# Loads back from DRAM set apart from their stores on one DMA queue, in a two-layer graph kernel

## The chip, the cores and the metric

The kernel runs on one core of a Trainium2 chip. The metric is the device time of one execution in microseconds (us), the median of several runs. The engines are named as in the profile: PE (matrix products), PEld (its weight loads), DVE, ACT and POOL (elementwise work), and SP, which does no arithmetic here and issues every DMA; SPq is its queue.

## The reference

128 graphs of 128 nodes with 256 features each go through two layers. All data are float32.

```python
# layer 0: two graph attention passes, then a feed-forward block
Wh = h @ W;  e = leaky_relu(Wh @ a1 + (Wh @ a2).T, 0.2)
att = softmax(where(adj > 0, e, NEG), axis=1);  h = att @ Wh          # twice
h = layernorm(x + h);  x = layernorm(h + relu(h @ wf1 + bf1) @ wf2 + bf2)
# layer 1: 8-head attention with one value matrix per relation r, then a feed-forward block
attn = softmax(q @ k.T / sqrt(32))
out = sum over r of (attn * (adj == r)) @ (x @ Wv[r] + bv[r])
x = layernorm(x + out @ Wo + bo)
return layernorm(x + gelu(x @ W1 + b1) @ W2 + b2)
```

The adjacency holds zeros and ones. A test on the device finds that and takes the arm of the program called `BINARY`, in which two of the four relations are enough.

## The kernel before

**Groups and stages.** Four graphs make a group (`G = 4`), and there are 32 groups. Each goes through five stages: `load`, `gat` (both attention passes of layer 0), `ff0`, `att` (the attention of layer 1) and `ff1`. A stage is a Python generator: it emits some instructions, yields a number, and is resumed later. The planner in `layers` keeps all generators in a heap, ordered by a time of its own: a group's stages begin at `PERIOD * g` plus a fixed offset (`begin`, 48 for `ff0`, 132 for `att`, 300 for `ff1`; the period is 100), and each yielded number is the distance to the next step. These numbers, in the table `TIMES`, are plan units and not microseconds. So several groups are in work at once, and the steps of different groups interleave.

**What the order of emission fixes.** SP's instructions stay in the order of emission throughout, PE's from plan time 280 on (`kept`). The order on DVE, ACT and POOL is chosen by the framework's scheduler, by priority and by its own estimate of times.[...]

**Trips through DRAM.** PE multiplies over partitions, so some tiles must be turned. In the first and the last group this is done by PE (`direct`). In the others DVE turns blocks of 32x32 in place, four stores write the tile to a DRAM buffer `zd` with the blocks in their new places, and one load brings it back (`transposed`, lines 288 to 293):

```python
nc.vector.transpose(z, y)
s = dr.tile([n, N, NQ, Q], F32, name="zd", bufs=8)
for i in range(NQ):
    nc.sync.dma_start(s[:, :, i]..., z[ts(i, Q)]...)
nc.sync.dma_start(t, s.rearrange("k p i t -> p k (i t)"))
```

The load waits for the four stores to have landed, on SP. A group makes seven such trips of 512 KB: features ahead of `ff0`, `att` and `ff1` (`features`, tile `T`), and the attention weights of its four graphs (`turned`, tile `e` to `eT`). A smaller trip spreads a row of layer 0's scores over all partitions, twice a group: one store to `zsd` and one load into `e` (`gat_weighting`, lines 405 and 407).

**The attention stage.** `weights(b)` makes the scores of graph b (L490), their row maxima (L496), exponentials (L500) and, on POOL, the division (L502). The plan then has `turned` for graph 0, a step of 5, `turned` for graph 1, a step of 5.5, then the values of graph 0 (`v`, PE L531 and DVE L532) and the masked weights (`m`, DVE L515, from `eT` and the mask `am`). `weighted` (L544, tile `av`) multiplies `v` with `eT` and `m`: the first product of a graph with the weights that made the trip. In the loop over the four graphs the values, output projection (L577), `turned` and `m` of later graphs follow one another.

**Around it.** POOL also does the gains and offsets of the layer norms (`affine`, L271), sums for the feed-forward blocks (L309 to L312, L352), and small steps of the norms (L259 to L263).

Of the kernel before, what the change touches and what calls it, by code (L numbers as in the profile page):

```python
# [24 lines left out]
P = 128  # L25
G = 4
# [2 lines left out]

TIMES = {  # L30
    "sums": 5, "ff visits": (2.5, 2.5, 3, 3, 3.25, 3.25, 3.25, 3.25), "ff2": 3,
    "ff first half": 10, "ff half": 5, "row": 16, "gat": 19, "wh": 5.5,
    "gat copy": 2, "qk": 4.5, "scores": 5.5, "turn0": 10, "turn1": 5,
    "v0": 5.5, "av": 9, "v": 4, "wo": 4, "turn": 3, "mask": 3,
    "lead ff0": 26, "lead att": 32, "lead ff1": 32, "affine": 7,
    "store": 25,
}
STAGES = "load", "gat", "ff0", "att", "ff1"
# [182 lines left out]
def stages_of(tc, a, out, c, pools, plan):  # L221

    nc = tc.nc
    TIMES, binary = plan["times"], plan["binary"]
# [6 lines left out]
    DC, R, MW = c.DC, c.R, c.MW  # L231
# [38 lines left out]
        for op, v in zip((OP.mult, OP.add), c.ln[k]):  # L270
            engine.tensor_tensor(y[:, b:b + n], y[:, b:b + n], v[:, None, :].to_broadcast([P, n, D]), op)  # L271

    def transposed(y, t, direct, z):

        n = y.shape[1]
        if direct:
            for k in range(0, n, G):
                p = ps.tile([P, G, N], F32, name="mm")  # L280
                for b in range(G):
                    nc.tensor.transpose(p[:, b], y[:, k + b], c.ident)  # L282
                if k:
                    nc.vector.tensor_copy(t[:, k:k + G], p)
                else:
                    nc.scalar.copy(t[:, k:k + G], p)
            return
        nc.vector.transpose(z, y)
        s = dr.tile([n, N, NQ, Q], F32, name="zd", bufs=8)
        for i in range(NQ):  # L290
            nc.sync.dma_start(s[:, :, i].rearrange("k (j a) t -> a (k j) t", a=Q),  # L291
                              z[ts(i, Q)].rearrange("a k (j t) -> a (k j) t", t=Q))
        nc.sync.dma_start(t, s.rearrange("k p i t -> p k (i t)"))

    def t_tile():
        return wk.tile([P, G * MW], F32, name="T", bufs=TB)[:, :G * D]
# [1 line left out]
    def features(y, direct):  # L298

        t = t_tile().rearrange("p (b c n) -> p b c n", b=G, c=DC)  # L300
        blocks = t.rearrange("p b c n -> p (b c) n")
        transposed(y.rearrange("p b (c f) -> p (b c) f", f=P), blocks, direct, blocks)
        return t

    def moving_sums(hT):
# [9 lines left out]
    def feed_forward(y, before, direct, win, bin_, wout, func, by=G):  # L315


        hT = features(y, direct)
        yield TIMES["lead ff0" if before == "01" else "lead ff1"]
        hs = moving_sums(hT)  # L320
        yield TIMES["sums"]
        fT = [None] * FC

        def unit(f0):

            lo, hi = (wk.tile([P, 2, 2, T // 2], F32, name="fT", bufs=FC // 2) for _ in range(2))
            for i in range(2):
                fT[f0 + i] = lo[:, i].rearrange("p h t -> p (h t)")
                fT[FC // 2 + f0 + i] = hi[:, i].rearrange("p h t -> p (h t)")

            def product(p, k, first=False):
                for i in range(2):
                    nc.tensor.matmul(p[:, i], win[k][:, ts(f0 + i, P)], hs[k], start=first and i == 0, stop=True,  # L333
                                     skip_group_check=True)

            chain, side = (ps.tile([P, 2, T // 2], F32, name="mm") for _ in range(2))
            product(chain, 1, True)
            product(side, 5, True)
            nc.scalar.copy(lo[:, :, 0], chain)
            nc.scalar.copy(hi[:, :, 0], side)  # L340
            yield
            p = ps.tile([P, 2, T // 2], F32, name="mm")
            product(chain, 6)
            product(p, 2, True)
            product(side, 3)
            nc.scalar.copy(lo[:, :, 1], chain)
            nc.vector.tensor_add(lo[:, :, 0], lo[:, :, 0], p)
            nc.vector.tensor_add(lo[:, :, 1], lo[:, :, 1], side)  # L348
            yield
            product(chain, 7)  # L350
            nc.scalar.copy(hi[:, :, 1], chain)  # L351
            nc.gpsimd.tensor_add(hi[:, :, 1], hi[:, :, 1], hi[:, :, 0])  # L352
            for i in range(2):
                nc.scalar.activation(lo[:, i], lo[:, i], func, bias=bin_[:, f0 + i:f0 + i + 1])  # L354
            yield
            product(chain, 4)
            for h, p in enumerate((chain, hi[:, :, 1])):
                for i in range(2):
                    f = FC // 2 + f0 + i
                    nc.scalar.activation(hi[:, i, h], p[:, i], func, bias=bin_[:, f:f + 1])  # L360
            yield

        units = [unit(0), unit(2)]
        for n, now in enumerate(((0,), (1,), (0,), (1,), (0,), (1,), (0,), (1,))):
            for u in now:
                next(units[u])
            if n in (2, 4):
                affine(y, before, n - 2, 2)
            yield TIMES["ff visits"][n]
        yield TIMES["ff2"]  # L370

        late = sorted(range(FC), key=lambda f: f % (FC // 2) // 2)
        ys = [ps.tile([P, 2, D], F32, name="mm") for _ in range(G // 2)]

        def second(b, part):

            for n, f in part:
                nc.tensor.matmul(ys[b // 2][:, b % 2], fT[f][:, ts(b, N)], wout[:, f],  # L378
                                 start=b % 2 == 0 and n == 0, stop=n == FC - 1, skip_group_check=True)

        order = list(enumerate(late))
        for b in range(G):
            second(b, order[:FC // 2])
        yield TIMES["ff first half"]
        for k in range(0, G, 2):
            for b in (k, k + 1):
                second(b, order[FC // 2:])
            nc.vector.tensor_add(y[:, k:k + 2], y[:, k:k + 2], ys[k // 2])
            yield TIMES["ff half"]
            if (k + 2) % by == 0:  # L390
                normalised(y, k + 2 - by, by)
        return y

    def gat_weighting(wh, k, cap, direct):

        e = wk.tile([P, G, N], F32, name="e")
        if direct:
            p = ps.tile([P, G, N], F32, name="mm")
            for b in range(G):
                nc.tensor.transpose(p[:, b], wh[:, b, k + 1:k + 2].to_broadcast([P, N]), c.ident)  # L400
        else:
            z = sm.tile([P, G, Q], F32, name="zs", bufs=2)
            nc.vector.transpose(z, wh[:, :, k + 1:k + 2].to_broadcast([P, G, Q]))
            s = dr.tile([G, NQ, Q], F32, name="zsd")
            nc.sync.dma_start(s.rearrange("b i t -> i b t"), z[::Q])
            p = e
            nc.sync.dma_start(p, bass.AP(tensor=s.tensor, offset=s.offset, ap=[[0, P], [1, G * N]]))
        yield TIMES["row"]
        for b in range(G):
            nc.scalar.activation(e[:, b], p[:, b], AF.Identity, bias=wh[:, b, k:k + 1])  # L410

        n = 2 if direct else G
        parts = [slice(b, b + n) for b in range(0, G, n)]
        nm = sm.tile([P, G], F32, name="nm")
        s = sm.tile([P, G], F32, name="s")
        for k in parts:
            nc.vector.scalar_tensor_tensor(e[:, k], e[:, k], ALPHA, e[:, k], op0=OP.mult, op1=OP.max)
            nc.vector.scalar_tensor_tensor(e[:, k], cap[:, k], BIG, e[:, k], op0=OP.subtract, op1=OP.min)
            nc.vector.tensor_reduce(nm[:, k], e[:, k], AX.X, OP.max, negate=True)  # L419
        for k in parts:  # L420
            for b in range(k.start, k.stop):
                nc.scalar.activation(e[:, b], e[:, b], AF.Exp, bias=nm[:, b:b + 1], accum_out=s[:, b:b + 1])  # L422
            nc.vector.reciprocal(s[:, k], s[:, k])  # L423
            nc.gpsimd.tensor_mul(e[:, k], e[:, k], per_row(s[:, k], N))  # L424
        return e
# [32 lines left out]

    def attention(y, g, first, direct):

        hT = features(y, first or direct)
        at = load_mask(g)
        yield TIMES["lead att"]
        qT = t_tile().rearrange("p (c t) -> p c t", c=DC)
        for i in range(DC):
            p = ps.tile([P, T], F32, name="mm")
# [37 lines left out]

        def turned(e):
            eT = wk.tile([P, H, N], F32, name="eT")
            transposed(e, eT, direct, e)
            return eT

        def by_relation(b, eT, parts):  # L510

# [45 lines left out]
        eT = [turned(es[0])]  # L557
        yield TIMES["turn1"]
        eT.append(turned(es[1]))
        yield TIMES["v0"]  # L560
        PARTS = range(R)
        v, ms = values(0), by_relation(0, eT[0], range(R))
        for b in range(G):
            more = b + 1 < G
            affine(y, "02", b, 1)
            yield TIMES["av"]
            oT = weighted(ms, v)

            if b + 2 < G:
# [11 lines left out]
                eT.append(turned(es[b + 2]))  # L581
            yield TIMES["mask"]
            if more:
                ms = by_relation(b + 1, eT[b + 1], range(R))
        yield 1
        normalised(y)
        return y
# [195 lines left out]
```

## Time and profile before

| | |
|---|---|
| time, median of 3 runs | 2887.8 us (2886.82 to 2892.35) |
| profiled execution, span | 2890.0 us, mean clock of PE 0.982 |
| busy | PE 2787.7, PEld 2166.1, ACT 1724.3, POOL 1597.4, DVE 1504.7 us |
| the 16 DMA engines | busy for 49% of the span, 113 GB/s |
| stores of trips | 496 of `e` and 364 of `T`, 128 KB each |
| loads of trips | 124 of `eT` and 91 of `T`, 512 KB each |
| SP's queue waiting for stores of `e`, `T`, `zs` to land | 327.3, 228.4 and 197.9 us |

A busy PE isn't a PE at its peak, since products overlap. The idle time of an engine matters only where it delays another that sets the end. In a timeline, each line gives the start, the length, the engine or queue, the line of the kernel, the operation, what it writes and reads, and in brackets how long the engine had stood idle and for what. The profile numbers tiles away, so `eT` stands for the tiles of all graphs.

### The profile page before, as it was taken

To read this page: it belongs to the slowest core of one execution; us is meant where nothing else is said; L and a number is where in the kernel's file an instruction comes from. 1 tells how busy PE (TensorE), PEld (TensorE's weight loads), DVE (VectorE), ACT (ScalarE), POOL (GpSimd) and SP (SyncE) were. 2 spreads that over 40 slices of the span, in tenths; PEclk is the share of its full clock that TensorE was granted. 3 is DMA by queue.
4 is the path that set the end of the run, shared out by engine and by line. 5 is a ranking of instruction groups with operands and counts; after the bars stand their busy time and mean duration, and the time that the engine had idled before them with its cause. 6 is when DMAs were issued, how large, how long until landed. Compare 5 with 4: busy or idle time off the path is not lost.

```text
span 2890.0 us, 45554 instructions
## 1 busy us (share of the span) xinstructions
PE 2787.7 (96%) x15554; PEld 2166.1 (75%) x15554; DVE 1504.7 (52%) x3072; ACT 1724.3 (60%) x5191; POOL 1597.4 (55%) x1866
## 2 busy tenths in 40 slices
PE   4996999999999999999999999999999999999988
PEld 3764777777877777777777787777778777777756
DVE  5444545545545555554554555555565545555442
ACT  3445566566666666666656666666666675666543
POOL 1434556556655556665655665565566565556553
PEclk7998999999999999999999999999999999999999
DMA  7145454555554556555445545454654544564310
GB/s 275 45 104 121 104 118 106 110 132 127 119 114 107 113 117 139 114 119 118 106 108 131 129 113 125 104 111 117 137 128 107 123 106 111 122 135 106 77 37 15
DMA packets 1156945, 328.69 MB, mean 114 GB/s; under 512 B 903008, under 2 KB 1126752, under 8 KB 1156064
## 3 DMA queue, kind: packets, MB, share of 16 engines
q1 hardware_dynamic: 1156704, 325.68, 49.1%
q8 instruction: 126, 2.06, 0.3%
q14 instruction: 115, 0.94, 0.1%
HBM read 195.97 MB, written 129.62 MB: 113 GB/s over the span
## 4 chain that ended last, share of the span: by engine, by line
PE 71%; DMA 7%; DVE 6%; POOL 5%; ACT 4%; issue 2%; SPq 2%; DVEq 0%; POOLq 0%; ACTq 0%
PE mm L378 25%; PE mm L333 19%; PE mm L531 5%; PE mm L474 4%; PE mm L468 4%; PE mm L490 4%; PE av L544 3%; PE mm L435 3%; PE mm L577 3%; POOL tok L271 2%; DMA zd<-e 2%; SPq L291 2%; DMA eT<-zd 2%; PE mm L454 1%; DMA zd<-T 1%
## 5 line engine op out<-in xcount | busy, mean ns | idle before, releaser
L271 POOL TENSOR_TENSOR tok<-tok,ln_rows 128x512 f32<-128x512 f32 (+1 forms) x596 | 669.5, 1133 | 34.4 <-PE mm L282 11.1
L500 ACT ACTIVATE e<-mm,nm 128x128 f32<-128x128 f32 x1024 | 362.1, 397 | 239.2 <-DVE nm L496 229.6
L378 PE MATMUL mm<-w,fT 128*128 128x256 f32 x2048 | 460.6, 381 | 0.0
L378 PE MATMUL mm<-wf,fT 128*128 128x256 f32 x2048 | 456.6, 381 | 1.5 <-ACT fT L354 1.5
L378 PEld LDWEIGHTS mm<-w,fT 128*128 128x128 f32 x2048 | 386.6, 190 | 74.2 <-issue 24.2
L502 POOL TENSOR_TENSOR e<-e,s 128x512 f32<-128x512 f32 x256 | 269.4, 1053 | 300.5 <-DVE s L501 299.8
L378 PEld LDWEIGHTS mm<-wf,fT 128*128 128x128 f32 x2048 | 386.5, 190 | 64.3 <-issue 9.2
L515 DVE TENSOR_TENSOR m<-eT,am 128x1024 f32<-128x1024 f32 x128 | 186.2, 1454 | 385.2 <-DMA eT<-zd 374.8
L496 DVE TENSOR_REDUCE nm<-mm 128x4 f32<-128x512 f32 x256 | 162.9, 676 | 254.6 <-PE mm L490 254.6
L265 ACT ACTIVATE tok<-tok,nmr,rstd 128x256 f32<-128x256 f32 x480 | 249.9, 603 | 20.1 <-POOL nmr L263 20.0
L531 PE MATMUL mm<-wv,T 128*128 128x512 f32 x512 | 249.3, 610 | 0.0
L352 POOL TENSOR_TENSOR fT<-fT 128x512 f32<-128x512 f32 x128 | 163.3, 1277 | 153.8 <-ACT fT L351 153.8
L500 ACT ACTIVATION_READ_ACCUMULATOR e<-mm,nm 128x1 f32 x1024 | 242.9, 237 | 0.0
L354 ACT ACTIVATE fT<-fT,col 128x512 f32<-128x512 f32 x256 | 170.4, 715 | 118.8 <-DVE fT L348 117.1
L309 POOL TENSOR_TENSOR t<-T 128x256 f32<-128x256 f32 x64 | 47.6, 744 | 321.3 <-DMA T<-zd 321.0
L333 PE MATMUL mm<-T,w 128*128 128x256 f32 x768 | 202.3, 386 | 4.0 <-DMA T<-zd 2.9
L424 POOL TENSOR_TENSOR e<-e,s 128x512 f32<-128x512 f32 (+1 forms) x68 | 68.1, 1002 | 244.4 <-DVE s L423 230.6
L333 PE MATMUL mm<-T,wf 128*128 128x256 f32 x768 | 193.1, 381 | 0.0
L256 DVE BATCH_NORM_STATS2 st<-tok 128x6 f32<-128x256 f32 x480 | 176.7, 409 | 2.4
L333 PEld LDWEIGHTS mm<-T,w 128*128 128x128 f32 x768 | 144.4, 192 | 30.6 <-issue 6.5
L422 ACT ACTIVATE e<-e,nm 128x128 f32<-128x128 f32 x256 | 101.6, 430 | 105.2 <-DVE nm L419 98.8
L333 PEld LDWEIGHTS mm<-T,wf 128*128 128x128 f32 x768 | 146.1, 191 | 21.7 <-issue 0.8
(144 smaller groups left out, 5147.1 us busy)
## 6 DMA issues: line engine op xcount, KB each, us to landing
zd<-e SPq DMA_DIRECT2D x496, 128.0 KB, 4.6
eT<-zd SPq DMA_DIRECT2D x124, 512.0 KB, 4.4
zd<-T SPq DMA_DIRECT2D x364, 128.0 KB, 3.5
T<-zd SPq DMA_DIRECT2D x91, 512.0 KB, 4.2
xt<-in_xT_dram SPq DMA_DIRECT2D x32, 512.0 KB, 5.0
e<-zsd SPq DMA_DIRECT2D x60, 256.0 KB, 3.3
tok<-in_x_dram SPq DMA_DIRECT2D x30, 512.0 KB
out_dram<-tok SPq DMA_DIRECT2D x29, 512.0 KB, 5.4
```

Source lines behind the costliest of these rows:

```text
L256: nc.vector.bn_stats(st, y[:, b])
L265: nc.scalar.activation(y[:, b], y[:, b], AF.Identity, bias=nmr[:, b:b + 1], scale=rstd[:, b:b + 1])
L271: engine.tensor_tensor(y[:, b:b + n], y[:, b:b + n], v[:, None, :].to_broadcast([P, n, D]), op)
L333: nc.tensor.matmul(p[:, i], win[k][:, ts(f0 + i, P)], hs[k], start=first and i == 0, stop=True, skip_group_check=True)
L352: nc.gpsimd.tensor_add(hi[:, :, 1], hi[:, :, 1], hi[:, :, 0])
L354: nc.scalar.activation(lo[:, i], lo[:, i], func, bias=bin_[:, f0 + i:f0 + i + 1])
L378: nc.tensor.matmul(ys[b // 2][:, b % 2], fT[f][:, ts(b, N)], wout[:, f], start=b % 2 == 0 and n == 0, stop=n == FC - 1, skip_group_check=True)
L496: nc.vector.tensor_reduce(nm, p, AX.X, OP.max, negate=True)
L500: nc.scalar.activation(eh[:, q], p[:, q], AF.Exp, bias=nm[:, q:q + 1], accum_out=s[:, q:q + 1])
L502: nc.gpsimd.tensor_mul(eh, eh, per_row(s, N))
L515: nc.vector.tensor_tensor(m, eT, at[:, b][:, None, :].to_broadcast([P, H, N]), OP.mult)
L531: nc.tensor.matmul(p, hT[:, b, f], wv[:, f, r:r + 2], start=f == 0, stop=f == DC - 1)
```

## The change

Each trip is emitted in two steps. `transposed` becomes `put`, which turns and stores, and a new `get` emits the load, 4 to 6 plan units later. The numbers in `TIMES` that followed a trip are smaller by what the new steps take, so that everything else keeps its plan time. The aim is that SP doesn't have to wait for the stores to land before it issues what comes next. In `attention` the load of graph 0 is emitted behind the stores of graph 1, that of graph 1 one step later; the loads of graphs 2 and 3 get a step of their own in the loop.

```diff
@@ -29,10 +29,10 @@
 
 TIMES = {
     "sums": 5, "ff visits": (2.5, 2.5, 3, 3, 3.25, 3.25, 3.25, 3.25), "ff2": 3,
-    "ff first half": 10, "ff half": 5, "row": 16, "gat": 19, "wh": 5.5,
+    "ff first half": 10, "ff half": 5, "row": 12, "gat": 19, "wh": 5.5,
     "gat copy": 2, "qk": 4.5, "scores": 5.5, "turn0": 10, "turn1": 5,
-    "v0": 5.5, "av": 9, "v": 4, "wo": 4, "turn": 3, "mask": 3,
-    "lead ff0": 26, "lead att": 32, "lead ff1": 32, "affine": 7,
+    "v0": 5.5, "av": 9, "get": 3, "put": 6, "row put": 4, "v": 4, "wo": 4, "turn": 3, "mask": 3,
+    "lead ff0": 20, "lead att": 26, "lead ff1": 26, "affine": 7,
     "store": 25,
 }
 STAGES = "load", "gat", "ff0", "att", "ff1"
@@ -270,7 +270,7 @@
         for op, v in zip((OP.mult, OP.add), c.ln[k]):
             engine.tensor_tensor(y[:, b:b + n], y[:, b:b + n], v[:, None, :].to_broadcast([P, n, D]), op)
 
-    def transposed(y, t, direct, z):
+    def put(y, t, direct, z):
 
 
 
@@ -284,13 +284,17 @@
                     nc.vector.tensor_copy(t[:, k:k + G], p)
                 else:
                     nc.scalar.copy(t[:, k:k + G], p)
-            return
+            return None
         nc.vector.transpose(z, y)
         s = dr.tile([n, N, NQ, Q], F32, name="zd", bufs=8)
         for i in range(NQ):
             nc.sync.dma_start(s[:, :, i].rearrange("k (j a) t -> a (k j) t", a=Q),
                               z[ts(i, Q)].rearrange("a k (j t) -> a (k j) t", t=Q))
-        nc.sync.dma_start(t, s.rearrange("k p i t -> p k (i t)"))
+        return s
+
+    def get(t, s):
+        if s is not None:
+            nc.sync.dma_start(t, s.rearrange("k p i t -> p k (i t)"))
 
     def t_tile():
         return wk.tile([P, G * MW], F32, name="T", bufs=TB)[:, :G * D]
@@ -299,7 +303,9 @@
 
         t = t_tile().rearrange("p (b c n) -> p b c n", b=G, c=DC)
         blocks = t.rearrange("p b c n -> p (b c) n")
-        transposed(y.rearrange("p b (c f) -> p (b c) f", f=P), blocks, direct, blocks)
+        s = put(y.rearrange("p b (c f) -> p (b c) f", f=P), blocks, direct, blocks)
+        yield TIMES["put"]
+        get(blocks, s)
         return t
 
     def moving_sums(hT):
@@ -315,7 +321,7 @@
     def feed_forward(y, before, direct, win, bin_, wout, func, by=G):
 
 
-        hT = features(y, direct)
+        hT = yield from features(y, direct)
         yield TIMES["lead ff0" if before == "01" else "lead ff1"]
         hs = moving_sums(hT)
         yield TIMES["sums"]
@@ -404,6 +410,7 @@
             s = dr.tile([G, NQ, Q], F32, name="zsd")
             nc.sync.dma_start(s.rearrange("b i t -> i b t"), z[::Q])
             p = e
+            yield TIMES["row put"]
             nc.sync.dma_start(p, bass.AP(tensor=s.tensor, offset=s.offset, ap=[[0, P], [1, G * N]]))
         yield TIMES["row"]
         for b in range(G):
@@ -458,7 +465,7 @@
 
     def attention(y, g, first, direct):
 
-        hT = features(y, first or direct)
+        hT = yield from features(y, first or direct)
         at = load_mask(g)
         yield TIMES["lead att"]
         qT = t_tile().rearrange("p (c t) -> p c t", c=DC)
@@ -504,8 +511,7 @@
 
         def turned(e):
             eT = wk.tile([P, H, N], F32, name="eT")
-            transposed(e, eT, direct, e)
-            return eT
+            return eT, put(e, eT, direct, e)
 
         def by_relation(b, eT, parts):
 
@@ -557,13 +563,18 @@
         eT = [turned(es[0])]
         yield TIMES["turn1"]
         eT.append(turned(es[1]))
+        get(*eT[0])
         yield TIMES["v0"]
+        get(*eT[1])
         PARTS = range(R)
-        v, ms = values(0), by_relation(0, eT[0], range(R))
+        v, ms = values(0), by_relation(0, eT[0][0], range(R))
         for b in range(G):
             more = b + 1 < G
             affine(y, "02", b, 1)
-            yield TIMES["av"]
+            if b and b + 1 < G:
+                yield TIMES["get"]
+                get(*eT[b + 1])
+            yield TIMES["av"] - (TIMES["get"] if b and b + 1 < G else 0)
             oT = weighted(ms, v)
 
             if b + 2 < G:
@@ -581,7 +592,7 @@
                 eT.append(turned(es[b + 2]))
             yield TIMES["mask"]
             if more:
-                ms = by_relation(b + 1, eT[b + 1], range(R))
+                ms = by_relation(b + 1, eT[b + 1][0], range(R))
         yield 1
         normalised(y)
         return y
```

## The prediction

> **What bounds the kernel now.** I read the busy table first, then busy time by stretches, then TensorE's waits, and last the timelines of one group (four graphs, about 85 us), engine by engine.
>
> ```profile
> PE 2787.7 (96%) x15554; PEld 2166.1 (75%) x15554; DVE 1504.7 (52%) x3072; ACT 1724.3 (60%) x5191; POOL 1597.4 (55%) x1866
> ```
>
> ```profile
> 150.00:250.00 100.00, 82.49 (x457) 55.27 (x456) 44.75 (x88) 46.07 (x161) 31.15 (x39) 0.91 0.48 103
> 1720.00:2580.00 860.00, 859.37 (x4842) 672.39 (x4841) 468.61 (x956) 540.14 (x1626) 507.25 (x587) 1.00 0.52 118
> ```
>
> The second fence gives the stretch, its length, and PE, PEld, DVE, ACT and POOL busy, the clock, the DMA share and GB/s. Between 1720 and 2580 us the PE is busy for 859.4 of 860 us at full clock; between 150 and 250 us, where the pipeline fills, it idles 17.5 us.
>
> ```profile
> PE av L544 <- DMA eT<-zd: 14.6, 2, 12.0
> ```
>
> ```profile
> PE av L544 <- DVE v L532: 2.8, 5, 0.6
> ```
>
> The waits of the PE (total, times, longest): the longest entry from 130 to 260 us, and the whole list from 400 to 2580 us. So in the steady part the PE waits at one place only, L544, the product of weights and values. By the PE's timeline the first `L468` of a group starts at 373.21 and, 27 groups later, at 2675.05 us: 85.25 a group. The undisturbed groups take 85.05, so all that the steady part can give back is 2301.84 - 27 x 85.05 = 5.5 us.
>
> That one place in an ordinary group (call A the start of `av` for the first graph, 1437.27), by the timelines of SP's queue, DVE, POOL and PE (start, us, queue or engine, line, operation):
>
> ```profile
> 1424.64 2.56 SPq L291 DMA_DIRECT2D zd<-e  x4
> 1430.01 0.38 SPq L293 DMA_DIRECT2D eT<-zd  x1
> 1430.49 4.21 SPq L291 DMA_DIRECT2D zd<-e  x4
> ```
>
> ```profile
> 1423.37 1.24 DVE L288 STREAM_TRANSPOSE e<-e 128x1024 f32<-128x1024 f32 x1
> ...
> 1426.29 1.21 DVE L288 STREAM_TRANSPOSE e<-e 128x1024 f32<-128x1024 f32 x1
> ...
> 1434.31 1.68 DVE L515 TENSOR_TENSOR m<-eT,am 128x1024 f32<-128x1024 f32 x1 [2.75 <-DMA eT<-zd]
> 1435.92 0.68 DVE L532 TENSOR_TENSOR v<-mm,bv 128x512 f32<-128x512 f32 x1
> ```
>
> ```profile
> 1434.87 2.27 POOL L271 TENSOR_TENSOR tok<-tok,ln_rows 128x512 f32<-128x512 f32 x1
> ```
>
> ```profile
> 1437.27 0.43 PE L544 MATMUL av<-eT,v 128*32 128x128 f32 x8
> ```
>
> DVE turns the first graph's weights at 1423.37, SP issues four stores, waits for them until 1430.01, issues the load; it lands at 1434.31 (the DVE product `m` starts). DVE's turn of the second graph is over at 1427.50 (1426.29 + 1.21), but its stores go out at 1430.49, because SP was waiting. The product ends at 1435.92, `v` follows, and `av` starts on time: `v` may start up to 0.74 before it (1522.95 - 1522.21 in the late group below), so at most at A - 0.74; it starts at A - 1.35. The margin is 0.61 us.
>
> Now one of the late groups, whose first stores landed late (A would be 1522.32):
>
> ```profile
> 1519.93 1.28 POOL L271 TENSOR_TENSOR tok<-tok,ln_rows 128x512 f32<-128x512 f32 x1
> 1521.16 1.19 POOL L263 TENSOR_TENSOR nmr<-nmr,rstd 128x4 f32<-128x4 f32 x1
> ```
>
> ```profile
> 1520.10 2.19 DVE L515 TENSOR_TENSOR m<-eT,am 128x1024 f32<-128x1024 f32 x1 [3.49 <-DMA eT<-zd]
> ```
>
> ```profile
> 1522.95 0.42 PE L544 MATMUL av<-eT,v 128*32 128x128 f32 x8 [0.56 <-DVE v L532]
> ```
>
> The load landed at A - 2.2 instead of A - 3.0, that is 0.7 later, but `m` ended 1.24 later, and the PE waited. The POOL lines say why: in the ordinary group `m` was there before POOL's `L271` began at A - 2.40 and POOL took 2.27 for an operation of 1.28; in the late group `L271` had begun, and `m` had to sit it out until A - 1.16. So the end of `m` is a staircase: landing before A - 2.40, no stall; up to about A - 1.0, 0.62 us; after that the next `L271` is in front and the stall is 0.62 + 0.2 + 1.28 = 2.1. Six of 28 groups are on the second step (`av` at 499.55, 585.37, 1011.71, 1522.95, 2119.37 and, past the window of the list above, 2630.43).
>
> [...] the second store group, issued at 1430.49, keeps the engines busy only after the load.[...] here four stores took 2.56 us into an empty queue and 4.21 behind a load.
>
> **The change, part by part.** Nothing is computed differently; the planner's sums stay (4 + 12 for the row, 6 + 20 and 6 + 26 for features, 3 + 6 for `av`), so PE, DVE, ACT and POOL are emitted in the same order. Only the place of the loads in SP's in-order queue moves. With the planner's times modulo a period of 100, SP's order now is: ff1 trip at 0, eT2 14.5, attention features 32, eT3 37.5, ff0 features 48, row one 60, eT0 84, eT1 89, row two 97 (plain loads and output stores keep their places; the mask's load stays behind the attention features). Trip loads move by 4 to 6. In between falls something in three places only; everywhere else the load still follows its stores directly and SP waits as before, at no cost or gain.
>
> (1) Row two: its load falls behind the ff1 stores, which wait for DVE's turn, in the next group over at A + 3.5 (1865.83 + 1.25). The load goes out at A + 3.5 + 2.6 = A + 6.1 instead of A + 5.6 and its data follow 3.75 us of store data: about 1 us later. Queued behind it: DVE `L417`, then `m` and `v` of the second graph, done at 1793.6 where the PE takes them at A + 18.66 = 1797.2. Hidden, with over 2 us to spare. The ff1 stores leave some 2.5 us earlier; the PE isn't waiting for them.
> (2) Attention features: the load goes behind eT3's stores. Their turn is done at 1810.12 when the feature stores' issue ends at 1811.20, so nothing is waited for; the load goes out near 1814.4 instead of 1813.41 and lands by 1820; `L468` reads it at 1823.09. Hidden. The ff0 trip moves up about 5 us, hidden too.
> (3) eT0's load goes behind eT1's stores. This is the one that reaches A. DMA share and GB/s in half microseconds (last two columns):
>
> ```profile
> 1425.50:1426.00 0.50, 0.50 (x4) 0.43 (x3) 0.50 (x3) 0.37 (x1) 0.50 (x1) 1.00 0.86 135
> ...
> 1429.00:1429.50 0.50, 0.50 (x4) 0.45 (x3) 0.50 (x3) 0.32 (x1) 0.50 (x2) 1.00 0.35 51
> ...
> 1432.50:1433.00 0.50, 0.50 (x3) 0.26 (x2) 0.00 (x0) 0.50 (x2) 0.50 (x2) 1.00 1.14 345
> ```
>
> Four stores keep the engines busy from 1425.5 to about 1429.25: 3.75 us. eT1's stores would go out from 1427.53, behind these, and be done at 1429.25 + 3.75 = 1433.0. The load's 0.524 MB at 340 GB/s (the rate at 1432.5) is 1.5 us more: 1434.5, and 0.6 to 0.75 until it is seen (1429.25 to 1430.01 for the stores): 1435.2. That is 0.9 us later than 1434.31. From below, if the load shares the engines instead of following the stores, 0.3; from above, issue of the stores at 4.21 and a landing of 4.3 to 5.2 after that, 1.8 to 2.6. I take 0.9: A - 3.0 becomes A - 2.1, over the edge at A - 2.40.
>
> Sum: of 22 groups now on time I let three quarters step over, as their landings scatter by 0.3: 16.5 x 0.62 = 10.2; the late groups then lose another 0.15 (periods of 85.83, not 85.67), 2.5; of the six late ones half go to the third step: 3 x 1.5 = 4.5. Together +17.
>
> **The start.** In group 1 SP put eT0's load out at 237.67 and eT1's at 245.11. With the change eT1's stores (turn over at 236.03) come first, eT0 lands about 0.9 later than 242.1, but eT1 at about 245.2 instead of 249.46, which frees DVE for `v` (a PE wait of 3.34), and row two goes 3 us earlier. Net -2.5; group 0 loses 0.3 to 0.5. Tail: the last group turns on the PE; group 30's ff1 trip has nothing in between, 0.
>
> So 2887.8 + 17 - 2.5 = 2902.
>
> **Rivals.** *Within 0.2%, 2886:* the load is late by less than 0.5 and stays below the first edge; only the start changes. For it: the edge is 0.3 us away from my value. Against: 3.75 us of stores are now ahead of it. *Faster, 2880:* with the loads later in the scheduler's own times it puts `v` before `m` on DVE, as in groups 0 and 1; then `m` may end at A and no stall is left: -5.5 - 2.5. The PE's order before planner time 280 isn't fixed and may move too, either way. Against: later groups all have `m` first, even in the second graph, where `v`'s inputs are there long before. *Much slower, 2945:* landings beyond A - 1.0, or `m` pushed behind `zs` on DVE, which waits for ACT until A + 0.26: 2.1 x 28 = 59. For it: the upper bound of 2.6. Against: it needs a full queue all the way.
>
> **Chances.** The forecast 0.52, within 0.2% 0.17, faster 0.21, much slower 0.10. A third-step share between forecast and the last case stretches the top to 2925; the faster case reaches 2879. Faster by over 0.2% (below 2882) 0.22, within 0.18, slower (above 2893.6) 0.60.
>
> **What would show it.** Right: in most groups eT1's stores issued before eT0's load, `m` starting after A - 2.40 behind a POOL `L271`, PE waits of 0.55 at L544 in 20 or more groups, periods of 85.8. SP's waits for store landings shrink by hundreds of us without a gain. Wrong: periods of 85.05 everywhere (edge not reached, or `v` first); waits at L468, L333 or L454 would mean that I judged (1) or (2) hidden falsely.

## The result, and the profile after

| | before | changed |
|---|---|---|
| time, median of 4 runs | 2889.2 us (2886.8 to 2892.4) | 2933.9 us (2921.0 to 2941.8) |
| ratio | | 1.015, 95% interval 1.0109 to 1.0191 |
| profiled execution, span | 2890.0 us | 2940.0 us, mean clock of PE 0.977 |
| first `q` product of group 3 (the fourth) | 373.21 us | 370.65 us |
| 27 groups from there, over 27 x 85.05 | 5.5 us | 50.9 us |
| from the 28th such product to the end | 214.95 us | 222.11 us |

The change costs 44.7 us, more than the 14 forecast and beyond the range. The last three rows add up to the 50.0 us between the two profiled executions: -2.6 + 45.4 + 7.2. The profiled execution of the changed kernel is the longest of the four. The shortest, of 2921.0 us, has a mean clock of 0.983, about that of before, so what is said below of the clock holds for the profiled execution and only in part for the median.

In the changed kernel the lines of the attention stage are: `L297` the load of a trip (L293 before), `L475` for `q` (L468), `L521` for `m` (L515), `L538` for `v` (L532), `L550` for `av` (L544); the stores stay at `L291`. The first line of its page with numbers, and the busy time by stretches (stretch, length, PE, PEld, DVE, ACT, POOL, clock, DMA share, GB/s):

```profile
PE 2801.4 (95%) x15554; PEld 2174.6 (74%) x15554; DVE 1515.3 (52%) x3072; ACT 1730.7 (59%) x5191; POOL 1621.6 (55%) x1866
```

```profile
400.00:1720.00 1320.00, 1294.34 (x7223) 1008.95 (x7222) 698.02 (x1426) 810.06 (x2433) 766.66 (x876) 0.99 0.52 115
1720.00:2580.00 860.00, 849.75 (x4795) 663.46 (x4794) 458.19 (x936) 537.27 (x1620) 507.31 (x579) 1.00 0.52 117
```

Two things are new against the kernel before. PE idles some 10 us in the second stretch, where it idled 0.6, and the clock is below 1 in the first. PE's waits from 400 to 2580 us still form a list of one line (total, times, longest):

```profile
PE av L550 <- DVE v L538: 35.9, 25, 3.1
```

It was 2.8 us in 5 waits. The place is the predicted one, and no wait at `q`, at the feed-forward products or at layer 0's products has appeared. The waits of SP's queue for stores to land (whole execution):

```profile
SPq L297 <- DMA zd<-e: 155.7, 167, 3.1
...
SPq L297 <- DMA zd<-T: 131.8, 123, 2.6
SPq L414 <- DMA zsd<-zs: 83.5, 31, 3.3
```

These were 327.3, 228.4 and 197.9 us. So the change does what it is for: SP waits 383 us less for stores. None of that shortens the steady part.

**An ordinary late group** (A, the time at which `av` would start, is 1812.49). The queue first, then lines of the timeline of all engines:

```profile
1799.86 6.37 SPq L291 DMA_DIRECT2D zd<-e  x8
1806.41 2.69 SPq L297 DMA_DIRECT2D eT<-zd  x2
```

```profile
1811.38 1.23 DVE L521 TENSOR_TENSOR m<-eT,am 128x1024 f32<-128x1024 f32 x1 [4.59 <-DMA eT<-zd]
1811.48 2.26 POOL L271 TENSOR_TENSOR tok<-tok,ln_rows 128x512 f32<-128x512 f32 x1
...
1812.53 0.68 DVE L538 TENSOR_TENSOR v<-mm,bv 128x512 f32<-128x512 f32 x1
...
1813.26 0.32 PE L550 MATMUL av<-eT,v 128*32 128x128 f32 x4 [0.70 <-DVE v L538]
```

All eight stores go out in one piece, and eT0's load at A - 6.1 behind them. It lands (read, as in the prediction, from the start of `m`) at A - 1.1, where the prediction has A - 2.1 and the kernel before A - 3.0. Here `m` slips in just ahead of POOL's `L271` (which takes 2.26 us in its place), `v` starts 0.04 after A, and PE is 0.77 late.

**A group on the third step** (A is 1196.21), from the same view:

```profile
1195.18 2.37 DVE L521 TENSOR_TENSOR m<-eT,am 128x1024 f32<-128x1024 f32 x1 [4.68 <-DMA eT<-zd]
1195.18 1.28 POOL L271 TENSOR_TENSOR tok<-tok,ln_rows 128x512 f32<-128x512 f32 x1
...
1196.41 2.26 POOL L358 TENSOR_TENSOR fT<-fT 128x512 f32<-128x512 f32 x1
1197.46 0.68 DVE L538 TENSOR_TENSOR v<-mm,bv 128x512 f32<-128x512 f32 x1
...
1198.20 0.32 PE L550 MATMUL av<-eT,v 128*32 128x128 f32 x4 [1.93 <-DVE v L538]
```

The load landed at A - 1.0, 0.1 later than in the group above. Here POOL's `L271`, which starts at the same 1195.18, took its 1.28 us, `m` took 2.37 instead of 1.23, and PE waits 1.93 us. Over the 27 groups, 13 are late by 0.60 to 0.82 us and 14 are on the third step (12 by 1.98 to 2.00, one by 2.35, one by 3.21): 38.7 us in all. The border lies between landings at A - 1.06 and A - 1.04, and the median landing is A - 1.04: the change has put the landing on the edge of the most expensive step.

**The other 12 us.** The two steps don't add up to 50.9. The rest is seen in the clock (the number after POOL's in such a line):

```profile
1199.00:1205.00 6.00, 6.00 (x34) 4.43 (x25) 2.32 (x5) 4.92 (x22) 3.19 (x4) 0.72 0.67 118
1288.00:1294.00 6.00, 6.00 (x24) 4.60 (x25) 2.01 (x5) 4.80 (x21) 3.25 (x4) 0.72 0.72 121
```

```profile
1643.00:1649.00 6.00, 6.00 (x33) 5.03 (x30) 1.92 (x6) 4.47 (x21) 3.85 (x5) 1.00 0.69 123
```

A mean of 0.72 over 6 us is 3.4 us at half clock (the trace's clock records have 0.50 from 1199.50 to 1202.91 us). Eight of the 14 third-step groups are followed by such a stretch, within a few us of `av`. Six of these have a period of 88.68 or 88.69 us where it would be 87.04 (the other two waited longer and have 88.98 and 89.91); the third line shows the same place of a group that has none. 8 x 1.65 = 13.2, and 38.7 + 13.2 = 51.9, against 50.9 measured (the last of the 27 periods is 0.4 shorter than 85.05 although it begins late). The kernel before has no such stretch between 400 and 2580 us. At the end it goes the same way once more: `av` waits 2.47 us until 2760.40, and the clock is 0.66 from 2757 to 2767 (6.8 us at half clock, worth at most 3.4). Together these are most of the 7.2 us there.

### The profile page after: what moved, and what is told of

Same layout as the page of the kernel before. It is cut to its first block, busy times and chain, and to the rows that moved or that the text cites. A ratio compares the mean times of both kernels' runs of the same rounds, so it can differ in the third digit from the quotient of the medians.

```text
span 2940.0 us, 45499 instructions
## 1 busy us (share of the span) xinstructions
PE 2801.4 (95%) x15554; PEld 2174.6 (74%) x15554; DVE 1515.3 (52%) x3072; ACT 1730.7 (59%) x5191; POOL 1621.6 (55%) x1866
## 4 chain that ended last, share of the span: by engine, by line
PE 83%; DMA 6%; DVE 4%; POOL 2%; issue 1%; SPq 1%; ACT 1%; DVEq 0%; POOLq 0%; ACTq 0%
PE mm L384 30%; PE mm L339 22%; DMA eT<-zd 5%; PE mm L537 5%; PE mm L497 5%; PE av L550 4%; PE mm L481 4%; PE mm L475 4%; PE mm L588 3%; PE mm L442 3%; PE mm L461 2%; DVE m L521 2%; SPq L291 1%; DVE v L538 1%; POOL tok L271 1%
## 5 line engine op out<-in xcount | busy, mean ns | idle before, releaser
L271 POOL TENSOR_TENSOR tok<-tok,ln_rows 128x512 f32<-128x512 f32 (+1 forms) x596 | 684.5, 1157 | 33.6 <-PE mm L282 11.4
L384 PE MATMUL mm<-wf,fT 128*128 128x256 f32 x2048 | 464.8, 385 | 1.5 <-ACT fT L360 1.5
L521 DVE TENSOR_TENSOR m<-eT,am 128x1024 f32<-128x1024 f32 x128 | 182.6, 1427 | 214.1 <-DMA eT<-zd 205.0
L358 POOL TENSOR_TENSOR fT<-fT 128x512 f32<-128x512 f32 x128 | 178.0, 1391 | 155.8 <-ACT fT L357 155.8
L288 DVE STREAM_TRANSPOSE e<-e 128x1024 f32<-128x1024 f32 x124 | 152.0, 1226 | 42.4 <-POOL e L509 42.4
L483 ACT ACTIVATE kbd<-mm,bk,own 128x512 f32<-128x512 f32 x128 | 92.5, 773 | 134.2 <-PE mm L481 134.2
L550 PE MATMUL av<-eT,v 128*32 128x128 f32 x2048 | 108.4, 283 | 60.8 <-DVE v L538 46.7
```

The costliest lines, as they stand in the source:

```text
L521: nc.vector.tensor_tensor(m, eT, at[:, b][:, None, :].to_broadcast([P, H, N]), OP.mult)
L550: nc.tensor.matmul(po[ts(q, DH), i], v[:, r, i * P + q * DH:i * P + (q + 1) * DH], ms[r][:, q // 2 * HC + i * 2 + q % 2], start=n == 0, st ...
```

## The experiments

The theory after the result: all of the loss comes from one load, eT0's, behind the stores of eT1; from its landing the staircase of `m` and POOL makes two lateness steps; and PE waits of 2 us bring the half clock. The rivals: another of the moved loads, or the other order that the scheduler gives DVE; a lateness without steps; transfers behind the load, not in front of it, as the cause of the late landing; a clock that falls with lateness itself or with something other than PE's idleness. "Over the floor" is the length of the 27 periods less 27 x 85.05.

**The load of graph 0 put back** (the change, all else kept):

```diff
         eT = [turned(es[0])]
+        get(*eT[0])
         yield TIMES["turn1"]
         eT.append(turned(es[1]))
-        get(*eT[0])
```

> The change with one line moved: the load of graph 0's turned weights (eT0) goes out straight behind its own stores again, ahead of eT1's stores; every other load stays where the change put it. My theory (eT0's load behind eT1's stores is the whole loss): eT0 lands near A - 3.0 again, periods of 85.05 to 85.8, at most one or two half-clock windows between 400 and 2500 us, and the 2.5 us gained in the start stay: 2884 to 2890 us. Rival (row two's load behind the ff1 stores, the features behind eT3's stores, or the order on DVE that the scheduler changed with them carry a good part): 2900 us or more, with eT0 landing on time.

Measured: 2891.26 us against 2891.51, ratio 0.9996 (0.9987 to 1.0005). 2.0 us over the floor, landings at A - 3.0, no half clock in the steady part. PE's waits from 400 to 2580 us, and a group that is on time (A is 1777.31):

```profile
PE av L550 <- DVE v L538: 2.2, 4, 0.6
```

```profile
1774.16 1.87 DVE L521 TENSOR_TENSOR m<-eT,am 128x1024 f32<-128x1024 f32 x1 [2.55 <-DMA eT<-zd]
1774.91 2.25 POOL L271 TENSOR_TENSOR tok<-tok,ln_rows 128x512 f32<-128x512 f32 x1
...
1775.95 0.68 DVE L538 TENSOR_TENSOR v<-mm,bv 128x512 f32<-128x512 f32 x1
```

All the other loads of the change stay moved, PE, DVE, ACT and POOL have the order of the changed kernel from 290 to 2750 us, and nothing is lost. So the loss is the place of one load. The time lies 1 us above the expectation, since the gain in the start went with it (first `q` product of group 3 at 374.17).

**That load alone** (the kernel before; `later` collects the loads of graphs 0 and 1; the lines that hand it down to `transposed` are left out here):

```diff
...
-        eT = [turned(es[0])]
+        later = []
+        eT = [turned(es[0], later)]
         yield TIMES["turn1"]
-        eT.append(turned(es[1]))
+        eT.append(turned(es[1], later))
+        for t, s in later:
+            nc.sync.dma_start(t, s.rearrange("k p i t -> p k (i t)"))
```

> The kernel before with only eT0's and eT1's loads moved behind eT1's stores; rows, features and the later graphs as before. My theory: most of the loss comes back, 2920 to 2945 us, av late by 0.6, 0.8 or 2.0 us in nearly all groups. Here eT1's load follows eT0's at once. Rival: below 2905 us, the rest belongs to the other moved loads.

Measured: 2923.5 us, ratio 1.0115 (1.0099 to 1.0132). Landings at A - 1.07 (median), 33.4 us over the floor, groups late by 0.60 to 0.81, 1.16 and 1.98 to 2.0. The swap of one load with four stores in the kernel before gives the steps of the changed one, with all engines in the order of before from 290 to 2750 us. In the profiled execution (2917.7 us, the shortest of four) no half clock follows, although 12 groups are late by 2.0. The first `q` product of group 3 comes at 366.61, 6.6 us earlier than before. That isn't shown to be the load's doing: with the swap the scheduler also gives PE another order from about 175 us on, and with the load put back PE has the order of before and no gain.

**Fewer POOL instructions** (the change; the gains and offsets that POOL applies inside `ff0`, of norm `01`, and behind `ff1`, of norm `12`, are left out, those of the last group's `12` kept):

```diff
-            if n in (2, 4):
+            if n in (2, 4) and before != "01":
                 affine(y, before, n - 2, 2)
...
-            affine(y, "12", b, 2, nc.vector if last else nc.gpsimd)
+            if last:
+                affine(y, "12", b, 2, nc.vector)
```

> The change without the gain and offset that POOL applies in ff0 (norm 01) and behind ff1 (norm 12; the last group keeps it): this part of the computation is left out, with these inputs (gain 1, offset 0) it changes no value. My theory (the masked product m waits its turn behind POOL's L271[...], so lateness comes in steps): m runs its 1.2 us from the moment eT0 lands, av is late by a continuous 0.5 to 1.6 us and by 0.9 on average, no half-clock windows in the steady part, 2900 to 2912 us. Rival (the lateness is that of the landing alone, POOL has no part in it): steps of 0.8 and 2.0 us stay, 2920 us or more.

Measured: 2913.05 us (one run). Landings stay at A - 1.03 (median), but the third step is gone. A group with the usual landing (A is 1788.61):

```profile
1786.46 1.27 POOL L358 TENSOR_TENSOR fT<-fT 128x512 f32<-128x512 f32 x1 [0.44 <-ACT fT L357]
...
1787.53 1.29 DVE L521 TENSOR_TENSOR m<-eT,am 128x1024 f32<-128x1024 f32 x1 [4.63 <-DMA eT<-zd]
...
1788.74 0.68 DVE L538 TENSOR_TENSOR v<-mm,bv 128x512 f32<-128x512 f32 x1
...
1789.47 0.32 PE L550 MATMUL av<-eT,v 128*32 128x128 f32 x4 [0.80 <-DVE v L538]
```

Behind POOL's last remaining `L358`, which ends at A - 0.9, `m` meets nothing more and ends 1.1 us later. 15 of 27 groups are late by 0.86 to 0.88, and all of them land before that end: one that lands at A - 1.74 has an `m` of 1.94 us and the same 0.86. Those that land later are, but for one, late by just as much as they land late, 0.97 to 1.60. No group is near 2.0, and no half clock occurs in the steady part. The time is 1 us above the expected range, and one step was left where none was expected. So the steps are POOL's instructions: with `L271` gone the third is gone, and with `L358` kept one is left.

**Values ahead of the masked weights** (the change; `v` is held ahead of `m` on DVE):

```diff
-        v, ms = values(0), by_relation(0, eT[0][0], range(R))
+        v = values(0)
+        added = nc.cur_bb.bb.instructions[-1]
+        ms = by_relation(0, eT[0][0], range(R))
+        tc.add_manual_dep(nc.cur_bb.bb.instructions[-1], added.name, mybir.DependencyInfo(
+            mybir.DependencyClass.NoSync, mybir.DependencyReason.DATA), reason="values first")
```

> The whole change, with v of graph 0 held ahead of m on DVE. My theory: groups in which m ends by A + 0.1 lose nothing, those where it ends at A + 1.25 lose 1.1 to 1.3 us instead of 2.0, no half-clock windows in the steady part: 2895 to 2912 us. Rival (the order of v and m has no part in it): 2920 to 2942 us.

Measured: 2897.82 us (one run). 12.1 us over the floor; nearly all periods are 85.05 or 86.22. The waits from 400 to 2580 us, and one group (A is 1781.08):

```profile
PE av L550 <- DVE m L521: 9.7, 10, 1.0
```

```profile
1777.72 0.69 DVE L538 TENSOR_TENSOR v<-mm,bv 128x512 f32<-128x512 f32 x1 [2.35 <-PE mm L537]
...
1779.98 1.22 DVE L521 TENSOR_TENSOR m<-eT,am 128x1024 f32<-128x1024 f32 x1 [1.57 <-DMA eT<-zd]
1780.06 2.29 POOL L271 TENSOR_TENSOR tok<-tok,ln_rows 128x512 f32<-128x512 f32 x1
...
1781.08 0.43 PE L550 MATMUL av<-eT,v 128*32 128x128 f32 x8
```

The landing is still at A - 1.1, but `v` no longer stands behind `m`: it starts at A - 3.36, as soon as its product is there (the line shows the wait for it), while in the late group of the changed kernel, behind `m`, it started at A + 0.04. The first `av` products read `eT` and `v` alone, so `m`, which ends at A + 0.1 here, holds up nobody in this group. Most of the loss is gone with the load still late. The same edit on the version with the load put back:

> The change with eT0's load back behind its own stores (as in e1_first_load_back), and on DVE the addition that makes v of graph 0 held ahead of the product m. My theory (av starts as soon as v and eT0 are there, m is needed only 0.24 us later, so a product that waits behind one POOL operation costs nothing): no waits of 0.6 us at av, periods of 85.05 throughout, some 4 to 5 us less than e1_first_load_back, 2884 to 2888 us. Rival (DVE loses as much in another place, or av waits for m): within 2 us of e1_first_load_back.

Measured: 2888.92 us (21 runs) against 2891.3 (25), ratio 0.9991 (0.9984 to 0.9998). PE waits nowhere between 400 and 2580 us, and the 27 periods are 0.7 us under 27 x 85.05: this is all that the steady part has to give. The gain over the version with the load put back is 2.3 us and not the 4 to 5 expected, since only 2.0 us over the floor were left there; the time is 0.9 above the range.

**Why the load lands so late: what stands behind it.** The load of graph 1 and the plain load of `tok` follow eT0's at once. First graph 1's load one step later (the change):

```diff
         yield TIMES["v0"]
-        get(*eT[1])
...
             yield TIMES["av"] - (TIMES["get"] if b and b + 1 < G else 0)
+            if b == 0:
+                get(*eT[1])
             oT = weighted(ms, v)
```

> The change with eT1's load emitted one step later, behind row two's and the ff1 stores, so that no load follows eT0's at once. Theory (part of eT0's late landing, 1.1 us from its last packet instead of 0.65, is due to the load of the same size right behind it): eT0 lands by A - 1.4, av late by 0.6 in most groups, 2900 to 2915 us. Rival (the late landing is that of the stores in front alone): eT0 lands at A - 1.1 as with the change, 2920 to 2942 us.

Measured: 2951.57 us (one run), and the theory behind this edit fell: eT0 lands at A - 0.64 (median), later than before the edit, 25 of 27 groups are on the third step, and eight half-clock stretches follow. The load of `tok` now comes directly behind eT0's. With that one moved as well, behind the second row's load:

```diff
-            nc.sync.dma_start(y, x[g])
         att = yield from gat_weighting(wh, D, cap, direct)
+        if not direct:
+            nc.sync.dma_start(y, x[g])
```

> As e6_second_load_later, and the plain load of tok, which went out right behind eT0's load there, is emitted after the second row instead, so that for 6 us nothing follows eT0's load on the queue. Theory (what is issued behind a load takes bandwidth from its last packets): eT0 lands at A - 1.5 or earlier, av late by 0.6 us in most groups, 2900 to 2918 us. Rival (the stores in front alone make it late): it lands at A - 1.1 to A - 0.7 as before, 2925 us or more.

Measured: 2924.23 us (one run), 34.7 us over the floor, landings at A - 1.13 (median; -1.04 in the changed kernel), 15 groups late by 0.60 to 0.79 and 12 by 2.0. The expectation (A - 1.5 or earlier, at most 2918 us) failed again: with nothing behind it the load is as late but for 0.1 us. So what follows the load is not why it is late here, though it can matter: with `tok` directly behind, it was 0.4 us later (3.7 us from first packet to landing). What is in front of it makes it late, and its own length. The rate of all DMA over 14 us in slices of 0.35 us, first the changed kernel from 1799 (A - 13.5), then the kernel before from 1424 (A - 13.3):

```profile
GB/s 0 0 0 0 10 137 142 145 163 109 129 169 162 150 134 129 149 153 146 139 90 167 165 150 144 154 140 176 199 331 329 269 167 176 256 287 334 391 367 351
```

```profile
GB/s 0 0 0 0 95 138 147 145 153 102 167 170 148 143 105 8 0 0 0 0 135 85 66 170 328 350 333 231 215 216 171 153 151 148 143 104 0 0 0 0
```

Above, 22 slices of about 145 GB/s are the eight stores (7.6 us, two of the 3.75 us predicted). The load follows without a gap, but its first slices have 176 and 199 GB/s, the last stores among them, then 331, 329 and 269. Below, where the load came to idle engines, it is slow first too: 135, 85, 66, 170, then 328 to 350. The trace's packets (512 bytes for loads, 128 for stores) give its length. From the first packet to the landing the median of 27 groups is 3.3 us in the kernel before, in the changed one, with the load alone moved, and with nothing behind it (3.32, 3.33, 3.30 and 3.32). The first packet moved from A - 6.3 to A - 4.4, and the landing with it. Where no other load follows, the last of the 1024 packets can be told: the data take 2.7 us before and 2.8 with nothing behind, and the landing follows 0.6 us later in both. Single loads scatter from 2.6 to 4.9 us.

**The half clock: PE's wait filled.** If idleness of PE brings the half clock, products without use in the place of the wait must take it away, with the lateness kept. In a first try two spare products of 128x512 stood ahead of the first `av`, in a buffer of the `mm` ring:

```diff
+            if b == 0:
+                spare = ps.tile([P, T], F32, name="mm")
+                for _ in range(2):
+                    nc.tensor.matmul(spare, c.ident, c.wv[:, 0, :T], start=True, stop=True)
             oT = weighted(ms, v)
```

> The whole change, with two spare products (128x512, result unused) on the PE ahead of av of graph 0, added work of about 0.9 us that runs in the wait. Theory (the half-clock windows come from an idle PE): no half-clock windows between 400 and 2700 us in spite of waits as long as before, mean clock 0.982 or more in all runs, 2915 to 2928 us with a spread under 8 us, although work was added. Rival (the windows have another cause, or the added work costs what it saves): clocks of 0.977 to 0.983 as with the change, 2930 us or more.

Measured: 2989.91 us, ratio 1.034 (1.0324 to 1.0356). It fills no wait: the spare products waited themselves, for the buffer that `v` is read from (25 waits, 40.5 us), and came on top of the wait (groups late by 2.5 to 5.7). The second try wrote four spare products of 128x256 into the bank of `av` itself, where they wait for nothing (`L546` below has no idle time ahead of it):

```diff
...
+            for _ in range(spare):
+                nc.tensor.matmul(po.rearrange("p c n -> p (c n)"), c.ident, c.wo[:, 0], start=True, stop=True)
...
-            oT = weighted(ms, v)
+            oT = weighted(ms, v, 0 if b else 4)
```

> The whole change, with four spare products (128x256, overwritten at once) on the PE ahead of av of graph 0, this time into av's own bank, so that they wait for nothing and run inside the wait (in e8 the spare ones waited for the same addition on DVE, through their PSUM buffer): 0.9 us of added work, 0 to 0.3 us of added time where the wait is 0.6. Theory (half-clock windows come where the PE has been idle for about 2 us): none between 400 and 2700 us, clock 0.982 or more in all runs, 2915 to 2930 us. Rival (another cause): clocks from 0.977 up as with the change, 2930 to 2945 us.

Measured: 2940.1 us (2939.2 to 2941.2), ratio 1.0162 (1.0146 to 1.0178). The stretches of the steady part, the waits from 400 to 2580 us, and one group (A is 1372.00; the spare products are `L546`):

```profile
400.00:1720.00 1320.00, 1316.77 (x7385) 1031.82 (x7384) 701.67 (x1434) 816.89 (x2449) 775.63 (x887) 1.00 0.52 116
1720.00:2580.00 860.00, 858.80 (x4843) 672.40 (x4842) 457.24 (x929) 530.84 (x1605) 498.52 (x567) 1.00 0.51 115
```

```profile
PE av L552 <- DVE v L538: 4.4, 16, 1.4
```

```profile
1371.91 1.89 PE L546 MATMUL av<-wo,ident 128*128 128x256 f32 x8
...
1374.00 0.42 PE L552 MATMUL av<-eT,v 128*32 128x128 f32 x8 [0.20 <-DVE v L538]
```

`v` and `av` are as late as in the changed kernel, 16 of 27 groups by 1.97 us or more, but PE works in between, and no half-clock stretch is left (1.00 in both lines). This agrees with PE's idleness as the cause, but proves less than it seems to. A wait of this length is followed by half clock only at some places of the clock's grid (last section), and by these places only one of the 16 groups, late by 3.2, would have been followed with its wait unfilled (four more begin between the borders given there). The load alone, with 12 groups as late and PE as idle and no such stretch, shows that neither lateness nor idleness is enough without the place. So that idleness is what counts there rests on that one group, and no other cause was tested apart; the cause of the half clock stays in part open. The time didn't fall as expected, because the spare products take 1.72 us and made the other 11 groups late by that much: 52.1 us of lateness and no clock loss here, 38.7 and 13.2 in the changed kernel. The four runs also agree within 2 us, where those of the changed kernel spread over 21; there the mean clock goes with the time (0.983 at 2921.0, 0.977 at 2938.4 and 2941.8).

**The swap where it helps** (the kernel before; loads of graphs 0 and 1 behind both groups of stores for groups 0 to 2 only, and `v` ahead of `m` in all):

```diff
...
-        eT = [turned(es[0])]
+        later = [] if g < 3 else None
+        eT = [turned(es[0], later)]
         yield TIMES["turn1"]
-        eT.append(turned(es[1]))
+        eT.append(turned(es[1], later))
+        for t, s in later or ():
+            nc.sync.dma_start(t, s.rearrange("k p i t -> p k (i t)"))
...
```

> The kernel before with two things: in groups 0 to 2 alone eT0's and eT1's loads follow eT1's stores (in e2_first_load_alone the first L468 after the start came 6.6 us earlier than in the kernel before), and v of graph 0 is held ahead of m on DVE throughout (as in e5). My theory (the order helps in the start, where the PE waits for eT1 too, and hurts in the steady part alone): start 5 to 7 us earlier, periods of 85.05, 2878 to 2884 us. Rival (the early start is lost again further on, or was another order on the engines by chance): 2886 to 2891 us.

Measured: 2886.97 us (2882.7 to 2890.4, 12 runs) against 2893.25 (16 runs), ratio 0.9976 (0.9968 to 0.9985): the shortest of all versions, and shorter than both kernels. It is above the 2878 to 2884 of the theory and where the rival has it. The first `q` product of group 3 is at 366.72, 6.5 us earlier than before, again with PE's other order in the start, so that the place of the loads and the order aren't told apart. Part of it is given back: two periods are 86.95 and 87.67, with waits that neither kernel has (400 to 2580 us):

```profile
PE mm L438 <- DVE fT L350: 1.5, 2, 0.8
PE mm L336 <- DVE tok L458: 1.2, 2, 1.0
PE mm L336 <- ACT fT L349: 0.6, 2, 0.3
```

Whether the other orders that the scheduler gave to DVE are the cause of these waits wasn't tried.

## Why the prediction was right in direction and wrong in size

- *Where PE waits.* Right. `av` of graph 0 is the only place in the steady part, and putting the one load back takes the whole loss away.
- *Parts (1) and (2), row two and the attention features hidden.* Right: no wait at `q` or at layer 0's products, and with all these loads still moved the time is that of before.
- *The start, -2.5.* The number is met, -2.56, but by luck. 1.05 us of it are there at 44 us already, before the first trip. PE's order before plan time 280, of which the prediction says that it may move either way, moved: at 175 us other products fill most of a wait of 2.68 us for group 0's first load (the first group's attention weights make the trip too). The wait that was to shrink because eT1 lands earlier has grown (kernel before, then changed):

```profile
253.81 0.43 PE L544 MATMUL av<-eT,v 128*32 128x128 f32 x8 [3.34 <-DVE v L532]
```

```profile
254.95 0.66 PE L550 MATMUL av<-eT,v 128*32 128x128 f32 x8 [5.36 <-DVE v L538]
```

What came as forecast is row two: the wait of 3.84 us for it at 263.36 is gone. The swap alone gives -6.6; what the other moved loads take back of that wasn't separated.
- *The staircase.* Right, steps and edges: 0.60 to 0.82 and 1.98 to 2.0 measured for 0.62 and 2.1, a border near A - 1.05 for "about A - 1.0". Taking POOL's instructions away removes the third step.
- *Part (3), the landing.* This is the step that failed, in the term "The load's 0.524 MB at 340 GB/s (the rate at 1432.5) is 1.5 us more". 340 GB/s is the rate of the load's second half. The slow first microsecond, which the trace of before has (135, 85, 66, 170), isn't in the term, and no reason is given. A load directly behind stores has it too: with the 0.6 to 0.75 until the load is seen, the prediction has 2.1 to 2.25 us from first packet to landing, and the measured median is 3.3, before as after. The 0.6 to 0.75 and the stores' 3.75 us were right. Why the load starts slowly stays open. So the load lands at A - 1.1 and not at A - 2.1, inside the bounds of the prediction (0.3 to 2.6 later, measured 1.9) but at the second edge and half of the time beyond it.
- *The sum.* With 3 of 28 groups forecast on the third step, 14 of 27 are there. That, the much slower rival's mechanism in half of the groups, makes 38.7 us of lateness where the forecast has 17 more than the 3.7 of before.
- *The clock.* Put at nothing in every case: about 13 us in the steady part of the profiled execution, and a part of the 7.2 at the end. In the trace of the changed kernel each of the eight stretches of the steady part is 3.41 us at half clock, all on one grid of 3.413 us, and PE waits of 1.92 to 1.93 us were enough for six of them (last section).
- *The range.* Its top, 2925, stretched the third-step share but held no cost of idleness beyond the idle time itself. Landings past A - 1.0 got one chance in ten, although none of the lines shown there has a load directly behind stores.

That POOL's instructions make the staircase is shown by the experiment with fewer of them: `m` takes 1.2 to 1.3 us in most groups there, against 1.7 to 2.4 in the third-step groups of the changed kernel. Why the two hold each other up wasn't shown.

## What to carry to other kernels

A queue that waits costs nothing unless what it delays is read soon: here SP waits 383 us less for stores, and the steady part gains nothing by it. Before moving a load behind other transfers, find its reader's margin and count the transfers put in front, and the load itself, at their measured length from first packet to landing (3.3 us for a load of 512 KB here) and not at a peak rate (1.5 us at 340 GB/s). Where an operand comes close to an edge of a staircase, price the far side too. A short wait of PE can cost more than its length (1.65 us on top of 1.93 here), so keep what PE needs first (here `v`) out of the queue behind what is late (here `m`).

## What the hardware showed that was not expected

- Waits of PE of 1.9 to 3.1 us were followed by 3.4 us at half clock in eight of 14 cases, and waits of 0.6 to 0.8 us in none of 13. The length doesn't decide between the 14; the place does. By the trace's clock records all half-clock stretches of one execution begin on one grid of 3.413 us. In the changed kernel, with the load alone moved, and in the two versions with later loads, PE waits 1.91 to 1.94 us 60 times between 390 and 2700 us. The 14 waits that begin from 0.05 us ahead of a grid point to 0.47 behind it are all followed by half clock, in the interval after the one that they lie in, and the 46 that begin 0.59 to 3.32 us behind it never are. The three longer waits (2.3 and twice 3.1 us) are all followed, the 45 shorter ones (up to 1.1 us) never. So less than 2 us of idleness at the beginning of an interval is enough. Why the place counts isn't shown, and the borders aren't the same everywhere: in the first try with spare products, where these and not `av` follow the wait, one that begins 0.88 behind a grid point is followed and one that begins 0.06 ahead isn't.
- Once it happens, it repeats: six periods in a row, of the groups from A = 1107.5 on, are 88.68 or 88.69 us, and 26 x 3.413 = 88.74, so the wait moves by only 0.05 us a group against the grid. It begins 0.24 us behind a grid point in the first of the six and 0.05 ahead of one in the last; in the next group, at 0.11 ahead, no half clock follows and the series ends.
- A 512 KB load of 512-byte packets took 3.3 us from first packet to landing (median) whether it came to idle engines or directly behind stores, with 66 to 199 GB/s in its first microsecond and about 330 to 350 later. Stores of the same size, in 128-byte packets, took 3.75 us, at about 140 GB/s.
